# W1's column product in four pieces around one score product, and a shorter run of products on constants

## The chip, the cores and the metric

The kernel runs on one core of one Trainium2 chip. The metric is the device time of one execution in microseconds (us), from a few runs of the same program; one further execution was profiled.

## The reference

32 graphs of 512 nodes with 256 features go through two layers, each followed by a residual sum and a normalization. Layer 0 is a whole transformer block under a symmetric mask; layer 1 is attention under the plain mask.

```python
# layer 0: x is (32, 512, 256), adj is (32, 512, 512); 8 heads of 32
allowed = (adj > 0) | (adj.swapaxes(1, 2) > 0) | eye
q, k, v = split(x @ Wqkv.T + bqkv)
attn = softmax(where(allowed, (q / sqrt(32)) @ k.T, -inf))
x1 = layernorm(x + (attn @ v) @ Wo.T + bo) * g1 + be1
ff = relu(x1 @ W1.T + b1) @ W2.T + b2          # 256 -> 1024 -> 256
x = layernorm(x + (layernorm(x1 + ff) * g2 + be2))
# layer 1
w = softmax(where(adj == 0, -inf, (q @ k.T) / sqrt(32)))
x = layernorm(x + (w @ v) @ Wo.T + bo)
```

## The kernel before

A graph stays in on-chip memory from its load to its store. The work of the 32 graphs overlaps like a pipeline, and its order is written out by hand: `opening` (line 658) starts graphs a to e, `period` (line 1552) is called 26 times for the steady part, and `closing` (line 1855) ends the last ones. Inside these functions each line is one step of one graph (`a.scores(0, 5)` is the score product of block 5 of layer 0 for graph a). The steps are issued in the written order, and each engine and each issuing queue works through its own part of that order strictly; a step waits only for the data and the buffers it needs.

The attention of a layer is cut into eight blocks: two groups of four heads, times four tiles of 128 keys. For a block, `scores` (line 475) makes 16 TensorE records that write a tile `s` of 128 x 2048 in PSUM, `exp` (line 484, ScalarE) turns it into a tile `p` in on-chip memory, `masked` (line 488, VectorE) multiplies by the mask, and `product` (line 495) sums the values. There is only one tile `s`, so the score product of a block waits until the exponential before it has read the last one. `sums` (line 519) makes the row sums of the first graph on TensorE.

A product in 32-bit floats appears in the trace as two records, and so does its weight load.

Three steps of the opening matter here:

- `warm` (line 326) is a run of products on a tile of ones. Their result goes to a PSUM bank `psW` that nothing reads. They need the memset of the constants and nothing else, and stand ahead of the first transposes (`psT`, line 436), which need the first graph's `x`.
- `once(2)` (line 381) multiplies W1 by the column of the bias b2, into the PSUM bank `psB`: eight slices of 128 outputs, two halves of the contraction each, 64 equal columns, so 16 products in all with a weight load of 128 x 128 each. `once_out(2)` (line 394) later subtracts the result from b1, since b2 is added elsewhere and has to be taken out of the hidden layer's bias. W1 is loaded by `constants(6, 8)`, on SyncE's queue; the next cast of an adjacency matrix on GpSimd's queue (line 338) is made to wait for that load.
- `once(0)` and `once(1)` (line 374) are two short products of the same kind for the other biases.

The order around them is: score product of block 4, exponential and mask of block 4, score product of block 5, exponential of block 5, `once(2)`, score product of block 6, and then the mask and exponential steps of blocks 5 and 6, three value products and block 7. The step `sort` between them issues small copies on SyncE's queue for the next graph.

Of the kernel before, what the change touches and what calls it, by code (L numbers as in the profile page):

```python
# [27 lines left out]
def kernel(ctx: ExitStack, tc: tile.TileContext, t: dict, out: bass.AP):  # L28
# [14 lines left out]
    B, N, D = x.shape  # L43
    P = 128
    NQ = N // P
# [4 lines left out]
    NF = DFF // P  # L50
# [12 lines left out]
    ones = const.tile([P, HD], F32, name="ones")  # L63
# [87 lines left out]
    def plain(pools: ExitStack):  # L151
# [78 lines left out]
        class Graph:  # L230
# [17 lines left out]
            def bank(self, kind, n, shape):  # L248
# [4 lines left out]
                    self.tiles[key] = ps_d.tile([P, *shape], F32, tag=f"d_{next(slots['d'])}", name=name, bufs=1)  # L253
                return self.tiles[key]

            def direct(self, layer):

                return (self.b, layer) in ((0, 0), (B - 1, 1))
# [62 lines left out]

            def warm(self):

                ps = self.bank("W", (0,), [N])
                for _ in range(4):
                    nc.tensor.matmul(
                        ps,
                        ones[:, 0:1].to_broadcast([P, P]),
                        ones[:, 0:1].to_broadcast([P, N]),
                        start=True,  # L330
                        stop=True,
                    )
# [33 lines left out]
                loads = [nc.sync.dma_start(out=dst, in_=src) for dst, src in resident[a:b]]  # L366
                first[a] = loads[0]

            def once(self, i):

                if i < 2:
                    bv, ps = proj[i][3], self.bank("B", (i,), [D])
                    for k in range(ND):
                        nc.tensor.matmul(
                            ps, bv[:, k : k + 1].to_broadcast([P, P]), wo[i][:, k, :], start=(k == 0), stop=(k == ND - 1)
                        )
                    return
                ps = self.bank("B", (i,), [NF, P // 2])
                for f in range(NF):
                    for c in range(ND):  # L380
                        nc.tensor.matmul(  # L381
                            ps[:, f, :],
                            w1[:, c, f * P : (f + 1) * P],
                            b2_c[:, c : c + 1].to_broadcast([P, P // 2]),
                            start=(c == 0),
                            stop=(c == ND - 1),
                        )
# [125 lines left out]
            def sums(self, layer, hg):  # L513

                ps = self.bank("R", (layer, hg), [N])
                folded = [2 + hg] if not self.direct(layer) else range(hg * NQ, (hg + 1) * NQ)
                for k in folded:
                    for j in range(HPC):
                        nc.tensor.matmul(  # L519
                            ps[j * HD : (j + 1) * HD, :],  # L520
                            ones,
                            self.p(layer, k)[:, j, :],
                            start=(k == folded[0]),
                            stop=(k == folded[-1]),
                        )
# [132 lines left out]
        def opening(a, b, c, d, e):  # L658
# [52 lines left out]
            a.exp(0, 4)  # L711
            a.masked(0, 4)
            b.sort(0, 1, 0)
            a.scores(0, 5)
            a.exp(0, 5)
            a.once(2)
            a.scores(0, 6)
            b.sort(0, 1, 1)
            a.masked(0, 5)
# [2035 lines left out]
        with tc.manual_schedule():  # L2755
            opening(*graphs[: 5])
            for k in range(1, 27):
                period(*graphs[k : k + 5])
            closing(*graphs[27 : 32])

    with ExitStack() as pools:
        plain(pools)
# [166 lines left out]
    with ExitStack() as pools:  # L2929
# [3 lines left out]
        ps = ps_f.tile([1, 1], F32, name="ps_total")  # L2933
# [36 lines left out]
```

## Time and profile before

| What | us |
| --- | --- |
| median of 3 runs | 2995.37 |
| lowest and highest of them | 2994.23, 2999.42 |
| profiled execution, its own time | 2996.1 |
| span of its trace, first to last instruction | 2994.3 |
| TensorE busy in the span | 2968.1 (99%) |
| VectorE busy | 2700.5 (90%) |
| ScalarE busy | 1747.3 (58%) |
| GpSimd busy | 998.8 (33%) |
| constants (`psW`), first record to the transposes | 1.09 to 6.47 |
| score product of block 5 | starts 29.10 |
| W1's column product (`psB`, 32 records) | 31.04, takes 7.09 |
| score product of block 6 | starts 38.06 |
| first query or key product of the second graph | starts 57.29 |

Times inside the trace are counted from its first instruction. Engines carry short names: PE is TensorE's products, PEld its weight loads, DVE VectorE, ACT ScalarE, POOL GpSimd, SP SyncE. A line of the timeline gives the start, the duration, the engine, the line of the kernel, the operation, what it writes and reads, how many records were merged, and in brackets the idle time before the first of them and who ended it. A line of the stretches gives the borders, the length, the busy time and the number of records for PE, PEld, DVE, ACT and POOL, then the mean clock that TensorE was granted as a share of the full one, the busy share of the DMA engines and the GB/s moved.

### The profile page before, as it was taken

The page shows a single profiled execution, that of the slowest core. Times are in us where ns is not written, and L with a number is a line of the kernel's source. Part 1 is how long each engine was busy: PE and PEld are TensorE (multiplying, and loading weights), DVE is VectorE, ACT ScalarE, POOL GpSimd, SP SyncE. Part 2 cuts the span into 40 slices and gives each one's busy share as a digit, 9 for nine tenths or more (in the row PEclk, how much of TensorE's full clock was granted, in tenths as well). Part 3 has the DMA queues.
Part 4 walks back from the last instruction along what each step waited for, and adds up shares of the span by engine and source line. Part 5 has one row for each costly group of instructions (what it writes and reads, how often), then busy time and mean ns, then how long its engine had stood idle before and what let it go on. Part 6 is the DMA issues. An engine that isn't in the chain of part 4 may idle for free.

```text
span 2994.3 us, 83802 instructions
## 1 busy us (share of the span) xinstructions
PE 2968.1 (99%) x36842; PEld 1371.5 (46%) x36842; DVE 2700.5 (90%) x3585; ACT 1747.3 (58%) x2111; POOL 998.8 (33%) x1247
## 2 busy tenths in 40 slices
PE   9999999999999999999999999999999999999997
PEld 3444444454444544444544445444444444454443
DVE  4889999999999999999999999999999999998996
ACT  4555665556656556655566565566555665655554
POOL 0333333323333323333233333233332333333332
PEclk9999999999999999999999999999999999999999
DMA  7566767767667766666676677666766766667550
GB/s 151 115 123 135 139 134 132 132 128 146 130 133 134 131 132 138 134 133 127 130 147 130 133 135 131 132 137 135 133 122 133 145 132 133 137 122 141 100 111 27
DMA packets 276436, 387.08 MB, mean 129 GB/s; under 512 B 153248, under 2 KB 237344, under 8 KB 245792
## 3 DMA queue, kind: packets, MB, share of 16 engines
q0 software_dynamic: 35744, 260.59, 47.2%
q1 hardware_dynamic: 240320, 121.05, 18.4%
q8 instruction: 291, 4.77, 0.6%
q14 instruction: 81, 0.66, 0.1%
HBM read 72.23 MB, written 33.55 MB: 35 GB/s over the span
## 4 chain that ended last, share of the span: by engine, by line
PE 96%; DVE 2%; ACT 1%; DMA 0%; issue 0%; POOL 0%; SPq 0%; DVEq 0%; POOLq 0%
PE s L475 18%; PE acc L495 15%; PE psH L162 15%; PE psF L162 14%; PE psQK_None L162 11%; PE psV L162 7%; PE psO L162 7%; PE psQK L162 4%; PE psT L436 2%; PE psR L519 2%; ACT p L484 1%; DMA p<-p 0%; DVE p L488 0%; DVE st L602 0%; PE psB L381 0%
## 5 line engine op out<-in xcount | busy, mean ns | idle before, releaser
L484 ACT ACTIVATE p<-s 128x2048 f32<-128x2048 f32 x512 | 963.4, 1882 | 493.4 <-PE s L475 487.9
L488 DVE TENSOR_TENSOR p<-p,m 128x2048 f32<-128x2048 f32 x512 | 1162.5, 2278 | 38.9 <-ACT p L484 35.4
L475 PE MATMUL s<-qT,kT 32*64 32x512 f32 x8192 | 572.1, 614 | 8.3 <-ACT p L484 4.5
L495 PE MATMUL acc<-p,v 128*32 128x512 f32 x4096 | 508.9, 597 | 0.0
L162 PE MATMUL psH<-xT,w_L_gnn_W 128*32 128x256 f32 (+1 forms) x6296 | 471.0, 380 | 0.0
L162 PE MATMUL psF<-w_L_gnn_W,hT 128*32 128x256 f32 (+1 forms) x6896 | 459.9, 380 | 0.0
L610 POOL TENSOR_SCALAR rs<-mv 128x2 f32<-128x2 f32 (+1 forms) x320 | 210.9, 659 | 686.6 <-DVE mv L605 668.1
L511 DVE TENSOR_TENSOR p<-p,p 128x2048 f32<-128x2048 f32 x186 | 424.1, 2281 | 4.2 <-DMA p<-p 3.0
L162 PEld LDWEIGHTS psH<-xT,w_L_gnn_W 128*32 128x32 f32 (+1 forms) x6296 | 300.3, 118 | 199.5 <-issue 54.7
L611 POOL TENSOR_TENSOR rs<-rs,neg_half 128x2 f32<-128x2 f32 (+1 forms) x320 | 374.0, 1169 | 26.7
L162 PEld LDWEIGHTS psF<-w_L_gnn_W,hT 128*32 128x32 f32 (+1 forms) x6896 | 286.6, 115 | 184.7 <-ACT hT L646 31.4
L508 POOL DMA_DIRECT2D p<-p x186 | 171.3, 921 | 497.5 <-PE acc L495 441.6
L646 ACT ACTIVATE hT<-psH,c_L_gnn_b 128x256 f32<-128x256 f32 x512 | 212.1, 474 | 193.7 <-PE psH L162 184.6
L475 PEld LDWEIGHTS s<-qT,kT 32*64 32x64 f32 x8192 | 119.4, 130 | 316.0 <-issue 111.0
L535 POOL DMA_DIRECT2D p<-p x124 | 106.9, 862 | 439.8 <-DVE mv L605 193.2
L162 PE MATMUL psQK_None<-xT,w_L_gnn_Wqkv 128*32 128x512 f32 (+1 forms) x1988 | 243.1, 594 | 0.7 <-ACT xT L441 0.7
L162 PE MATMUL psO<-w_L_gnn_Wo,cT 128*32 128x256 f32 (+1 forms) x2728 | 240.1, 380 | 1.8 <-DVE cT L581 1.8
L495 PEld LDWEIGHTS acc<-p,v 128*32 128x32 f32 x4096 | 118.9, 110 | 258.5 <-issue 193.7
L162 PEld LDWEIGHTS psO<-w_L_gnn_Wo,cT 128*32 128x32 f32 (+1 forms) x2728 | 154.5, 123 | 97.2 <-issue 43.0
L441 ACT COPY xT<-psT 128x512 f32<-128x512 f32 x130 | 76.0, 585 | 200.7 <-PE psT L436 200.7
L631 ACT ACTIVATE x<-z,ms,rs 128x256 f32<-128x256 f32 x128 | 73.1, 596 | 158.8 <-DVE ms L615 155.7
L602 DVE BATCH_NORM_STATS2 st<-y 128x6 f32<-128x256 f32 x384 | 155.0, 422 | 6.5
(79 smaller groups left out, 2876.3 us busy)
## 6 DMA issues: line engine op xcount, KB each, us to landing
p<-p POOLq DMA_DIRECT2D x186, 1024.0 KB, 7.8
p<-p POOLq DMA_DIRECT2D x62, 512.0 KB, 5.9
x<-in_x_dram SPq DMA_DIRECT2D x32, 512.0 KB, 4.2
code<-in_adj_dram POOLq DMA_DIRECT2D x32, 512.0 KB, 6.2
m<-code SPq DMA_DIRECT2D x32, 512.0 KB, 4.9
kT<-v SPq DMA_DIRECT2D x248, 64.0 KB, 4.2
p<-p POOLq DMA_DIRECT2D x62, 256.0 KB, 6.3
part<-p SPq DMA_DIRECT2D x248, 64.0 KB, 2.0
```

Source lines behind the costliest of these rows:

```text
L162: nc.tensor.matmul(out[at], lhsT[:, at], rhs, start=start, stop=stop)
L475: nc.tensor.matmul(s[half * P // 2 : (half + 1) * P // 2, j, :], self.kT(layer)[at, hg, key : key + P // 2], self.qT(layer)[at, hg, :], st ...
L484: nc.scalar.activation(self.p(layer, k), self.at("s", (layer, k), [HPC, N]), AF.Exp, scale=SCALE)
L488: nc.vector.tensor_tensor(p, p, m[:, k % NQ, None, :].to_broadcast([P, HPC, N]), ALU.mult)
L495: nc.tensor.matmul(acc[j * HD : (j + 1) * HD, :], self.v(layer)[:, kc, h * HD : (h + 1) * HD], self.p(layer, k)[:, j, :], start=(kc == 0), ...
L508: nc.gpsimd.dma_start(out=self.p(layer, k), in_=self.p(layer, k + 1), accum_op=ALU.add)
L511: nc.vector.tensor_tensor(self.p(layer, dst), self.p(layer, a), self.p(layer, b), ALU.add)
L535: nc.gpsimd.dma_start(out=p[:rows], in_=p[rows : 2 * rows], accum_op=ALU.add)
L602: nc.vector.bn_stats(self.at("st", (n, i), [6]), self.y(n, i))
L610: nc.gpsimd.tensor_scalar(rs, self.mv(n)[:, a:b, 1:2], EPS, None, ALU.add)
L611: nc.gpsimd.tensor_tensor(rs, rs, neg_half[:, a:b, None], ALU.pow)
L646: nc.scalar.activation(self.hT(h)[:, f, :], ps[:, f % 2, :], AF.Relu, bias=b1[:, f : f + 1])
```

## The change

`warm` issues nine products of 128 columns where it issued four of 512. `once` takes a piece of a quarter: pieces 0 and 1 of W1's column product are issued ahead of the score product of block 5, pieces 2 and 3 right behind it. The arithmetic of W1's product is the same. `sums` gets a step of its range through a new method that always returns 1, which leaves it as it was.

```diff
+            def step(self, layer, hg):
+
+                return 1
+
...
             def warm(self):
 
-                ps = self.bank("W", (0,), [N])
-                for _ in range(4):
+                ps = self.bank("W", (0,), [P])
+                for _ in range(9):
                     nc.tensor.matmul(
                         ps,
                         ones[:, 0:1].to_broadcast([P, P]),
-                        ones[:, 0:1].to_broadcast([P, N]),
+                        ones[:, 0:1].to_broadcast([P, P]),
                         start=True,
                         stop=True,
                     )
...
-            def once(self, i):
+            def once(self, i, piece=0):
...
-                for f in range(NF):
+                for f in range(piece * NF // 4, (piece + 1) * NF // 4):
                     for c in range(ND):
                         nc.tensor.matmul(
                             ps[:, f, :],
...
-                folded = [2 + hg] if not self.direct(layer) else range(hg * NQ, (hg + 1) * NQ)
+                folded = [2 + hg] if not self.direct(layer) else range(hg * NQ, (hg + 1) * NQ, self.step(layer, hg))
...
             a.exp(0, 4)
             a.masked(0, 4)
             b.sort(0, 1, 0)
+            a.once(2, 0)
+            a.once(2, 1)
             a.scores(0, 5)
+            a.once(2, 2)
+            a.once(2, 3)
             a.exp(0, 5)
-            a.once(2)
             a.scores(0, 6)
             b.sort(0, 1, 1)
             a.masked(0, 5)
```

## The prediction

> **What bounds the kernel now.** I read the busy shares and the chain first, then the granted clock in stretches, then the opening instruction by instruction.
>
> ```profile
> PE 2968.1 (99%) x36842; PEld 1371.5 (46%) x36842; DVE 2700.5 (90%) x3585; ACT 1747.3 (58%) x2111; POOL 998.8 (33%) x1247
> ...
> PE 96%; DVE 2%; ACT 1%; DMA 0%; issue 0%; POOL 0%; SPq 0%; DVEq 0%; POOLq 0%
> ```
>
> TensorE (PE) sets the end. From the busy time by stretches, once the opening is over there is no gap left in which a late start could be made good, or an early one lost:
>
> ```profile
> 120.00:2920.00 2800.00, 2797.85 (x34895) 1293.66 (x34897) 2584.44 (x3407) 1658.27 (x2003) 959.71 (x1180) 1.00 0.68 132
> ```
>
> So a microsecond that the opening gives TensorE should come out at the end. The change touches two places of the opening. The first is where the clock halves. Columns: stretch, its length, then busy time of PE, PEld, DVE, ACT, POOL, then the granted clock. I found the borders by cutting the trace finer and finer:
>
> ```profile
> 25.31:28.72 3.41, 1.12 (x16) 0.24 (x16) 3.41 (x3) 2.61 (x3) 0.52 (x1) 1.00 1.43 275
> 28.72:42.38 13.66, 13.28 (x76) 8.16 (x80) 8.61 (x5) 4.08 (x3) 0.00 (x0) 0.50 0.58 156
> 42.38:45.79 3.41, 3.41 (x40) 0.76 (x36) 2.00 (x1) 0.70 (x1) 0.00 (x0) 1.00 1.06 316
> ```
>
> In the 3.41 us up to 28.72 TensorE works 1.12 us; then its clock is 0.50 for 13.66 us, four times 3.41. The timeline shows why it was idle and what then ran slowly:
>
> ```profile
> 25.95 1.12 PE L475 MATMUL s<-qT,kT 32*64 32x512 f32 x16 [0.81 <-ACT kT L465]
> 29.10 2.02 PE L475 MATMUL s<-qT,kT 32*64 32x512 f32 x16 [2.03 <-ACT p L484]
> 31.04 7.09 PE L381 MATMUL psB<-c_L_gnn_b,w_L_gnn_W 128*128 128x64 f32 x32
> 38.06 2.01 PE L475 MATMUL s<-qT,kT 32*64 32x512 f32 x16
> 40.01 3.93 PE L495 MATMUL acc<-p,v 128*32 128x512 f32 x24
> 43.87 1.11 PE L475 MATMUL s<-qT,kT 32*64 32x512 f32 x16
> ```
>
> The score product of block 5 waits 2.03 us for the exponential of block 4 (one score tile); only behind it come the 32 records of W1's column product (psB), which need nothing of it. The same score product takes 1.12 us at full clock and 2.02 us at half.
>
> The second place is the run on constants that opens TensorE's work:
>
> ```profile
> 1.09 5.54 PE L326 MATMUL psW<-ones 128*128 128x512 f32 x8 [1.09 <-POOL total L66]
> ...
> 3.81 0.33 PEld L326 LDWEIGHTS psW<-ones 128*128 128x128 f32 x1 [0.52 <-issue]
> 4.67 0.27 PEld L326 LDWEIGHTS psW<-ones 128*128 128x128 f32 x1 [0.52 <-issue]
> 5.18 0.19 PEld L326 LDWEIGHTS psW<-ones 128*128 128x128 f32 x1 [0.24 <-issue]
> 5.61 0.19 PEld L326 LDWEIGHTS psW<-ones 128*128 128x128 f32 x1 [0.24 <-issue]
> ...
> 6.47 1.03 PE L436 MATMUL psT<-ident,x 128*128 128x128 f32 x8
> ...
> 8.23 3.70 PE L162 MATMUL psQK_None<-xT,w_L_gnn_Wqkv 128*128 128x512 f32 x8 [0.73 <-ACT xT L441]
> ```
>
> Its loads are 0.86 us apart up to 4.67 and 0.43 us from 5.18: the array starts at half clock and gets the full one near 4.8, though the clock column, which has no record before that, says 1.00.
>
> **What the Trainium skill says.** "TensorE: Matmul & The Clock Gate", Part 1 (the HAM clock gate): half clock is the idle default, and a free-running window of 3413 ns decides it. The trace agrees with the window (13.66 us is four of them; 4.8 lies seven before 28.72). The page asks for an idle window before the clock drops; here one with 1.12 us of work was enough, so the measurement decides: the border lies above a third busy. As the window isn't tied to the kernel's start, other executions may cut it elsewhere. Same page, Part 4 (PE-mode transpose): transposes don't count as busy in the same way. In the closing, 2936.85 to 2940.27 holds 1.70 us of busy time, half of it transposes (0.33 + 0.55), and the clock is 0.50 in the 3.41 us after it; 2981.23 to 2984.64 holds 1.70 us of plain products, and the clock stays up in the 3.41 us after it. That fits, and puts the border between 33% and 50% of plain products.
>
> **The pieces, step by step.** Only TensorE's order changes; the same 32 records of psB run, 16 ahead of the score product of block 5 and 16 behind it. No other engine or queue has an instruction moved, no bank is taken in another order. One record costs 7.02/32 = 0.219 us at half clock (chain: 31.11 to 38.13). I halve it: 0.110; the upper bound is 0.129, from the transposes (1.03/8, the same 128x128 load with twice the columns). So 16 take 1.76 to 2.06 us; I take 1.76. In the old timeline's numbers, at full clock:
> - block 4's scores end at 27.0; 16 records to 28.8, where 2.03 us were idle. Block 5 still starts at 29.1, since ACT's exponential (1.88 us from 27.17) is what it waits for; with 0.129 it moves by under 0.1.
> - Block 5's scores, 1.05 (12.71 to 13.76), to 30.15; 16 records to 31.9. The exponential of block 5 runs 30.3 to 32.2, so block 6 starts at 32.25: a new gap of 0.34 us. Before: 38.06.
> - Block 6's scores to 33.3; 24 records of products at 3.46/32 each (50.40 to 53.86), 2.6, to 35.9; block 7 to 36.95 (its exponential before it ended at 35.4); 8 records, 0.9, to 37.8; sums 3.54 (45.80 to 49.34) to 41.35; psB of L374 1.06 to 42.4; products 3.46 to 45.9; sums 3.43 to 49.3. There the next graph's query product starts, before at 57.29.
>
> The sum is 8.0 us: 6.6 from the clock, 1.4 from the filled gap. Does cover hold? DVE's masking is one run from 23.74 to 37.04 (six tiles at 2.2), tied to its mask's landing, not to TensorE. Tiles 6 and 7 follow to 39.3 and 41.6, and their products start at 44.1 and 45.0. W1 has landed by 25.41, when the cast that waits for it is let go; b2's column, issued at 5.71, long before. The sync queue issues to 45.6 without waiting for TensorE, then waits 8.5 us for its products; that wait shrinks, and the later loads move with it. What is late next: exponential 5, for 0.34 us.
>
> **The constants, step by step.** Four products of 512 columns (8 records) become nine of 128 (18 records). At half clock one costs between 0.22 (a 128-column load, from psB) and 0.258 (twice a transpose's): 3.96 to 4.64 us, so the run ends between 5.0 and 5.7, not 6.63. x, issued at 0.74 with 4.1 us to land, is there at 4.8. Transposes to first query product took 6.63 to 8.23, 1.6: so 6.7 to 7.3, with Wqkv landing near 6.9 (1.24 + 5.7). Gain 0.9 to 1.3; I take 1.1. The bound on the other side: if the shorter run (4.0 to 4.6 us, little more than one window) fails to fill a window, transposes cost 1.0 more, of which the copies leave about 0.5, and the 3.7 us of query products run at half for at least one window, 1.7 lost: 1.1 gained becomes about 1.1 to 1.7 lost. With the window where this profile had it (1.42 to 4.83), the run covers it.
>
> **Sum.** The profiled execution took 2996.1 us (span 2994.3, 1.8 around it), 0.7 above the median of 2995.37. 2996.1 - 8.0 - 1.1 = 2987.0. A clock drop of one window in the closing (1.7 us) may come or go as the window falls; it stays in the range.
>
> **Rivals.**
> - The run on constants is too short, the clock stays at half into the query products: 2996.1 - 8.0 + 1.6 = 2989.7. For it: a run of little over one window fills a free-running one only where it happens to fit. Against: most fits leave a window largely busy.
> - The pieces count too little and the clock drops all the same. They stream 64 columns against a load of 128, and windows full of them at half clock (32.14 to 38.96) did not raise it. But then psB ends near 33.2 instead of 38.1 and the products raise the clock one or two windows earlier: gain 4.1 to 5.8 of the pieces, 2990 with the constants. Against: each window now also holds one score product, 1.05 us, and 0.9 us of streamed pieces, over 50%.
> - The gain is lost later, to a load or a mask tied to time: half of it, 2992. Against: TensorE never waits from 29.10 to 117.98.
> - Slower: the pieces meet W1's transfer. They had 5.6 us of slack (31.04 against 25.41); now they start at 25.9 to 27.0, 0.5 to 1.6 after it, and TensorE takes its instructions in order, so block 5's scores, its exponential and mask stand behind the wait. DMA is dense here (0.98 to 1.07 of the engines in 20 to 30 us). W1 landing 9 us later eats the gain, 16 us later (41) makes it over 0.2% slower: about 3003. It would take a transfer three times as long as seen.
>
> **How the numbers follow.** A measurement of this kernel tells about 0.2%, 6 us, from no change: faster means below 2989.4. Forecast 0.60; clock low at the start 0.18, a third of it still below 2989.4; pieces don't hold the clock 0.10, a fifth below; lost later 0.07; slower 0.05. Faster 0.65, same 0.30, slower 0.05. The range runs from 2984.5 (forecast less the closing's drop and the shorter bounds) to 2992 (the first three rivals).
>
> **What would show it.** Right: no stretch of clock 0.5 between 25 and 45 us, 16 records of psB in some 1.8 us on either side of block 5's scores, block 6's near 31 to 32, the next graph's query product near 48. The constants: transposes from 5.0 to 5.7, loads in the query products 0.43 apart. Wrong: loads 0.86 apart there; half clock after the pieces; a wait of psB for W1; new TensorE waits between 45 and 120 us.

## The result, and the profile after

The changed kernel takes 2986.60 us (median of 10 runs, 2984.82 to 2989.85); the kernel before, in 10 runs, 2994.96 us. The ratio is 0.9972, 95% interval 0.9962 to 0.9981: 0.28% faster, with 0.2 to 0.4% in the interval. The forecast was 2987.0. A few executions of several of the kernels here, the kernel before among them, took 5 to 16 us more than their median, and so medians are compared. The profiled execution took 2986.66 us, with a span of 2984.9 against 2994.3. The mean granted clock of every timed run is on record: 0.998 or 0.999 in the ten of the changed kernel, 0.994 to 0.997 in all 96 of the kernel before that were timed for the experiments.

The opening by TensorE's timeline (start, duration, what, records, wait before), in the changed kernel (most of the same steps stand four lines further down in it, L475 at L479 for one):

```profile
1.09 4.21 PE L330 MATMUL psW<-ones 128*128 128x128 f32 x18 [1.09 <-POOL total L66]
5.09 1.38 PE L440 MATMUL psT<-ident,x 128*128 128x128 f32 x8
7.20 3.70 PE L162 MATMUL psQK_None<-xT,w_L_gnn_Wqkv 128*128 128x512 f32 x8 [0.73 <-ACT xT L445]
...
24.91 1.12 PE L479 MATMUL s<-qT,kT 32*64 32x512 f32 x16 [0.81 <-ACT kT L469]
25.96 2.00 PE L385 MATMUL psB<-c_L_gnn_b,w_L_gnn_W 128*128 128x64 f32 x16
28.07 1.12 PE L479 MATMUL s<-qT,kT 32*64 32x512 f32 x16
29.11 2.00 PE L385 MATMUL psB<-c_L_gnn_b,w_L_gnn_W 128*128 128x64 f32 x16
31.22 1.12 PE L479 MATMUL s<-qT,kT 32*64 32x512 f32 x16
32.27 2.78 PE L499 MATMUL acc<-p,v 128*32 128x512 f32 x24
...
48.40 3.62 PE L162 MATMUL psQK_None<-xT,w_L_gnn_Wqkv 128*32 128x512 f32 x32
```

The score product of block 6 starts at 31.22 instead of 38.06, and each of these score products takes 1.12 us: none is slow any more. The next graph's query product starts at 48.40 instead of 57.29, 8.9 us earlier. The clock in the windows of 3.41 us around the pieces (length, PE, PEld, DVE, ACT, POOL busy, then the clock):

```profile
22.88:26.29 3.41, 2.60 (x31) 0.70 (x23) 3.27 (x4) 2.61 (x4) 0.52 (x1) 1.00 1.15 290
26.29:29.70 3.41, 3.31 (x36) 2.36 (x36) 3.41 (x3) 2.14 (x2) 0.00 (x0) 1.00 1.30 243
29.70:33.12 3.42, 3.31 (x37) 1.80 (x40) 3.42 (x3) 2.15 (x2) 0.00 (x0) 1.00 0.39 115
```

None of these windows is under 76% busy, and the clock stays 1.00. Now follow the 8.9 us to the end. The closing of the changed kernel:

```profile
2925.13 1.95 PE L162 MATMUL psO<-w_L_gnn_Wo,cT 128*128 128x256 f32 x8
...
2932.27 1.13 PE L162 MATMUL psQK<-xT,w_L_gnn_Wk 128*128 128x256 f32 x4 [0.68 <-ACT xT L445]
2933.24 1.03 PE L162 MATMUL psQK<-xT,w_L_gnn_Wq 128*128 128x256 f32 x4
2934.83 1.12 PE L479 MATMUL s<-qT,kT 32*64 32x512 f32 x16 [0.56 <-ACT qT L469]
```

And of the kernel before:

```profile
2932.95 1.96 PE L162 MATMUL psO<-w_L_gnn_Wo,cT 128*128 128x256 f32 x8
...
2940.10 1.92 PE L162 MATMUL psQK<-xT,w_L_gnn_Wk 128*128 128x256 f32 x4 [0.67 <-ACT xT L441]
2941.81 1.91 PE L162 MATMUL psQK<-xT,w_L_gnn_Wq 128*128 128x256 f32 x4
2944.29 1.12 PE L475 MATMUL s<-qT,kT 32*64 32x512 f32 x16 [0.56 <-ACT qT L465]
```

The psO products are 7.8 us apart: 1.1 us were given back on the way, 0.9 of it where an earlier psO product waits for cT. In the changed kernel:

```profile
2882.30 1.93 PE L162 MATMUL psO<-w_L_gnn_Wo,cT 128*32 128x256 f32 x32 [1.71 <-DVE cT L585]
```

In the kernel before:

```profile
2890.13 1.93 PE L162 MATMUL psO<-w_L_gnn_Wo,cT 128*32 128x256 f32 x32 [0.77 <-DVE cT L581]
```

This wait was 1.69 and 1.75 us in two more profiles of the changed kernel and 1.09 in one more of the kernel before, so it is no accident of one execution; why it grew was not followed up. The score products are 9.5 us apart: the two query and key products ahead of them ran at half clock in the kernel before (1.92 and 1.91 us) and do not here. So 9.4 us of span are 8.9 from the opening, 1.7 from the closing's clock, less 1.1 (rounded). The medians are only 8.4 us apart. The closing's clock depends on where the windows fall: it halved in five of all twelve traces (the kernel before twice, the constants alone, one piece in the gap, five constants) and held in seven.

### The profile page after: what moved, and what is told of

Its sections match the earlier page's. It is cut to its first block, busy times and chain, and to the rows that moved or that the text cites. A ratio compares the mean times of both kernels' runs of the same rounds, so it can differ in the third digit from the quotient of the medians.

```text
span 2984.9 us, 83822 instructions
## 1 busy us (share of the span) xinstructions
PE 2959.3 (99%) x36852; PEld 1369.0 (46%) x36852; DVE 2700.2 (90%) x3585; ACT 1748.9 (59%) x2111; POOL 1002.0 (34%) x1247
## 4 chain that ended last, share of the span: by engine, by line
PE 95%; DVE 2%; ACT 1%; DMA 1%; issue 0%; POOL 0%; SPq 0%; DVEq 0%; POOLq 0%
PE s L479 18%; PE acc L499 15%; PE psH L162 15%; PE psF L162 15%; PE psQK_None L162 11%; PE psV L162 7%; PE psO L162 7%; PE psQK L162 4%; PE psT L440 2%; PE psR L523 2%; ACT p L488 1%; DMA p<-p 1%; DVE st L606 0%; DVE p L515 0%; DVE y L603 0%
## 5 line engine op out<-in xcount | busy, mean ns | idle before, releaser
L479 PE MATMUL s<-qT,kT 32*64 32x512 f32 x8192 | 570.4, 613 | 6.8 <-ACT p L488 2.7
L479 PEld LDWEIGHTS s<-qT,kT 32*64 32x64 f32 x8192 | 119.2, 129 | 313.5 <-issue 109.3
```

The lines of the kernel that those rows point to most:

```text
L479: nc.tensor.matmul(s[half * P // 2 : (half + 1) * P // 2, j, :], self.kT(layer)[at, hg, key : key + P // 2], self.qT(layer)[at, hg, :], st ...
```

## The experiments

The kernels were timed beside the kernel before, on the same chip for each group; "before" is its median there. In the diffs, the base is the changed kernel; "constants as before" stands for four products of 512 columns.

**The pieces alone.** Constants as before.

```diff
-                ps = self.bank("W", (0,), [P])
-                for _ in range(9):
+                ps = self.bank("W", (0,), [N])
+                for _ in range(4):
...
-                        ones[:, 0:1].to_broadcast([P, P]),
+                        ones[:, 0:1].to_broadcast([P, N]),
```

> The pieces as in the changed kernel, the constants as before (4 products of 512 columns). Theory (the pieces keep the full clock through the gap, and the constants add about 1 us of their own): no half clock between 25 and 45 us, the second graph's first query product near 49.3 instead of 57.29, time 8.0 us below the kernel before, about 2987. Rival (the early start of the whole opening by the shorter constants is what moved the idle gap against the clock's windows and kept the clock): the clock still halves after 28 us and at most 1.4 us are gained.

2986.89 us, before 2995.12, ratio 0.9971 (0.9961 to 0.9981). The trace has no half clock in the opening. Its query product starts at 50.26; its first transposes started at 7.30 instead of 6.47, so the pieces themselves gave 7.03 + 0.83 = 7.9 us (57.29 less 50.26, and the later start). The mean clock is 0.999 in all nine runs. The rival falls: the pieces carry the gain without the constants.

**The constants alone.** The whole product behind block 5.

```diff
-            a.once(2, 0)
-            a.once(2, 1)
             a.scores(0, 5)
+            a.exp(0, 5)
+            a.once(2, 0)
+            a.once(2, 1)
             a.once(2, 2)
             a.once(2, 3)
-            a.exp(0, 5)
```

> The constants as in the changed kernel, W1's column product whole and behind block 5 as before. Theory: the first query product starts 1.0 us earlier, the clock still halves once in the opening for two to four windows of 3.41 us, time 0.5 to 1.5 us below the kernel before. Rival (constants decide): no half clock, 7 to 9 us gained.

2993.71 us, before 2995.12, ratio 0.9995 (0.9986 to 1.0003). The clock stretches of its trace:

```profile
26.77:30.18 3.41, 1.93 (x24) 1.12 (x24) 3.41 (x2) 2.14 (x2) 0.00 (x0) 1.00 1.22 230
30.18:40.42 10.24, 10.24 (x59) 6.38 (x61) 8.12 (x5) 3.05 (x2) 0.00 (x0) 0.50 0.64 166
```

The clock halves for three windows. Three of the 13 runs took 2988.2 to 2988.4 us, all others 2993.3 or more. The mean granted clock on record is 0.999 in these three and 0.996 or 0.997 in the other ten. So with the constants alone the clock held in some executions and fell in most, and where it held the time was some 5 us shorter, about what three windows at half clock cost (half of 10.24 us). No trace of one of the three was taken.

**The whole product ahead of block 5.** Constants as before.

```diff
             a.once(2, 0)
             a.once(2, 1)
+            a.once(2, 2)
+            a.once(2, 3)
             a.scores(0, 5)
-            a.once(2, 2)
-            a.once(2, 3)
             a.exp(0, 5)
```

> Constants as before; all four pieces of W1's column product ahead of the score product of block 5, so that the gap before block 5 is overfilled and an idle gap of about 2.1 us arises before block 6, behind one score product and dense products after it. Theory (a window with little product work halves the clock, wherever it is): block 5 starts near 30.9 instead of 29.1, block 6 near 34.1 instead of 32.3; 1.8 us lost against the split pieces; if a window falls on the new gap the clock halves for one window and 1.7 us more are lost. 6.2 or 4.5 us below the kernel before. Rival (only that the product stands ahead of block 5 matters, not the split): the full 8.0 us.

2989.41 us, before 2995.12, ratio 0.9988 (0.9977 to 0.9999). The trace shows the gap moved by one block, and the clock falling there for one window:

```profile
31.79:35.21 3.42, 1.52 (x23) 0.41 (x27) 3.42 (x2) 2.15 (x2) 0.00 (x0) 1.00 0.42 119
35.21:38.62 3.41, 3.41 (x24) 0.82 (x16) 3.41 (x3) 1.58 (x1) 0.00 (x0) 0.50 0.75 208
```

Its timeline: block 5 starts at 30.54 and block 6, after 2.04 us of waiting, at 33.69; the 24 value products behind it take 4.48 us instead of 2.78. The query product starts at 52.57, 4.7 us before the old time, as the case with one halved window said. The split matters: with all records ahead, TensorE has nothing to do beside the exponential of block 5.

**Mere filling.** Constants as before; the first half of the product runs in the gap as well and again in its old place.

```diff
             a.once(2, 0)
             a.once(2, 1)
             a.scores(0, 5)
+            a.exp(0, 5)
+            a.once(2, 0)
+            a.once(2, 1)
             a.once(2, 2)
             a.once(2, 3)
-            a.exp(0, 5)
```

> Constants as before; the first half of W1's column product is issued twice, once ahead of block 5 as mere filling and again with the whole product behind block 5 where it was. Theory (6.6 of the 8.0 us are the clock's): the clock stays full, block 6 starts near 34.2, 1.9 us later than with the split pieces; about 6.1 us below the kernel before although TensorE does 16 records more. Rival (the gain is useful work moved into the gap): nothing gained, 0 to 1.8 us lost.

2990.73 us, before 2995.12, ratio 0.9988 (0.9980 to 0.9996); the profiled execution took 2989.16. TensorE's timeline of it:

```profile
26.88 2.00 PE L385 MATMUL psB<-c_L_gnn_b,w_L_gnn_W 128*128 128x64 f32 x16
28.98 1.12 PE L479 MATMUL s<-qT,kT 32*64 32x512 f32 x16
30.03 3.79 PE L385 MATMUL psB<-c_L_gnn_b,w_L_gnn_W 128*128 128x64 f32 x32
33.75 1.11 PE L479 MATMUL s<-qT,kT 32*64 32x512 f32 x16
```

The 16 extra records do no new work, and yet block 6 starts at 33.75 instead of 38.06 and the query product at 50.93, 6.4 us earlier (0.1 of it because this execution's opening began earlier). The old place of the product costs 3.7 us where it had cost 7.0. So most of the gain in the opening is the clock's; useful work in the gap is worth only the rest. The timed median is 4.4 us below the kernel before, with an interval of 1.2 to 6.0 us that just misses the 6.1 that were expected; the clear gain still rules out the rival.

**One piece in the gap.** Constants as before.

```diff
             a.once(2, 0)
-            a.once(2, 1)
             a.scores(0, 5)
+            a.once(2, 1)
             a.once(2, 2)
```

> Constants as before; only one of the four pieces (8 records, 1.0 us) ahead of block 5, three behind it, so that 1.0 us of the 2.03 us gap stays idle. Theory (the clock falls when too little product work lies in one window): the window on the gap holds one score product and one piece, more than the window that halved the clock in the kernel before; the clock holds, block 6 starts 0.9 us later than with two pieces on either side, about 7 us below the kernel before. If the clock falls in spite of the one piece: 2 to 4 us below, and the border lies above such a window.

2987.98 us, before 2994.49, ratio 0.9978 (0.9969 to 0.9986). The window on the gap and the next:

```profile
26.03:29.44 3.41, 2.15 (x24) 1.20 (x24) 3.41 (x3) 2.57 (x3) 0.00 (x0) 1.00 1.27 240
29.44:32.85 3.41, 3.41 (x37) 2.60 (x38) 3.41 (x2) 1.88 (x1) 0.00 (x0) 1.00 0.41 119
```

One microsecond of light products, with 1.0 us still idle, was enough in this execution: 63% busy, and the clock holds. The timed gain is 6.5 us, where about 7 were expected.

**A run on constants that is too short.** Five products instead of nine.

```diff
-                for _ in range(9):
+                for _ in range(5):
```

> The changed kernel with five products of 128 columns in the run on constants instead of nine (about 2.2 us of work at half clock, less than one window of 3.41 us). Theory (the run is there to lift the clock, and nine are about the least that does): the run ends near 3.3 us, the transposes start with x near 4.8 us but run at half clock, the query products start near 8 us instead of 7.2 and run at half for at least a window; 2 to 4 us above the changed kernel, 4 to 6 below the kernel before. Rival (the constants only delay the start): as fast as the changed kernel or up to 0.3 us faster.

2988.38 us, before 2994.49, ratio 0.9979 (0.9970 to 0.9988). Loads of the first query product, in time:

```profile
9.36 0.34 PEld L162 LDWEIGHTS psQK_None<-xT,w_L_gnn_Wqkv 128*128 128x128 f32 x1 [0.52 <-issue]
10.21 0.34 PEld L162 LDWEIGHTS psQK_None<-xT,w_L_gnn_Wqkv 128*128 128x128 f32 x1 [0.52 <-issue]
11.07 0.34 PEld L162 LDWEIGHTS psQK_None<-xT,w_L_gnn_Wqkv 128*128 128x128 f32 x1 [0.52 <-issue]
11.92 0.28 PEld L162 LDWEIGHTS psQK_None<-xT,w_L_gnn_Wqkv 128*128 128x128 f32 x1 [0.52 <-issue]
12.44 0.19 PEld L162 LDWEIGHTS psQK_None<-xT,w_L_gnn_Wqkv 128*128 128x128 f32 x1 [0.24 <-issue]
```

They are 0.85 apart until 11.9: the array is at half clock until 12.1. The transposes start at 4.88, when x has landed, but the first score product only at 14.24, against 11.68 in the changed kernel: 2.6 us lost. The run is there to lift the clock. In the timed runs the loss is smaller than the 2 to 4 us that were expected: the median is 1.3 to 1.8 us above those of the changed kernel (2986.60 and 2987.06 us, timed in other groups), and the intervals of the ratios overlap.

**Both kernels profiled once more**, for another cut of the windows.

> The kernel before, profiled once more. Theory (free-running windows of 3.41 us cut each execution elsewhere, but the idle gap before block 5 is long enough for most cuts): the clock halves again after 27 to 31 us, for two to four windows; the end of the run on constants moves by up to 1.5 us with the window.

> The changed kernel, profiled once more. Theory: no half clock between 25 and 45 us, wherever the window falls; the transposes start between 5.0 and 5.7 us; if the window does not fit the short run on constants, the query products start at half clock and the opening is 1 to 3 us later than in the first profile.

The kernel before halves again, from 30.16 to 43.81, after a window of 40%:

```profile
26.74:30.16 3.42, 1.39 (x24) 0.40 (x32) 3.42 (x2) 2.22 (x2) 0.00 (x0) 1.00 1.11 218
30.16:43.81 13.65, 13.65 (x80) 8.02 (x68) 8.42 (x5) 3.75 (x2) 0.00 (x0) 0.50 0.62 178
```

Its constants end 0.7 us later than in the first profile (transposes at 7.18). The changed kernel again has no half clock in the opening; its query product starts at 48.61.

**The closing filled.** Five products on constants into the gaps ahead of and behind the last transposes, and the changed kernel beside it.

```diff
+            e.fill(2)
             e.transpose(2, 1)
...
+            e.fill(3)
             e.query_key(1, 1, 0, 1, wide=True)
```

> The changed kernel, with five products of 128 columns on constants added in the idle gaps of the closing around the last transposes: two ahead of the last graph's second transposes of layer 1, three ahead of its key product after them (10 records, about 1.1 us, into the score tile that is empty there). Theory (too little product work in a window halves the clock, and some executions have such a window in the closing, which costs 1.65 us there): the clock stays full to the last products in every execution, nothing is delayed; the median falls by up to 1.7 us against the changed kernel, by as much as the share of executions that had the halving. Rival (the closing's halving is rare or is not from the gaps): no difference, or 0.1 to 0.5 us lost to the fillings.

> The changed kernel once more, beside the one with the filled closing on the same chip. 2986 to 2987 us; no half clock in the opening; in the closing the clock halves or not as the window falls.

2986.66 and 2987.06 us, before 2994.57; ratios 0.9980 (0.9970 to 0.9990) and 0.9976 (0.9970 to 0.9983). No difference that can be told. The closing of the changed kernel kept its clock in all three of its profiles without the fillings. Two kernels with the same closing lost it there, the one with one piece and the one with five constants, after windows of 50% and 54%, so the fillings have something to save in some executions; the timed runs don't show it. None of the versions is faster than the changed kernel by more than the noise.

Not every execution of these two kernels keeps its clock: in five of their 35 runs the mean clock is 0.997, and these five took 2992.4 to 2998.5 us. None of them was profiled. Three of them have the closing filled, so the gaps that were filled are hardly the cause. The shorter run on constants is no likely one either: the 11 runs with five constants have no such case, and the 13 with mere filling, on the old run, have one. Where the clock fell in them stays open.

## Why the prediction was right

**The pieces: right.** Forecast 8.0 us; 7.9 with the old constants. The steps held one by one: block 6 at 32.25 less the earlier start is 31.2, measured 31.22; the new gap before it shrank from 0.34 to 0.25 us (29.11 plus 1.86 is 30.97), since 16 records take 1.86 us, not 1.76: 32 of them run in 3.72 us in the two experiments with whole products, 0.116 each, inside the bounds of 0.110 and 0.129. Masks, context copies and the sync queue did not hold TensorE up in the opening, as argued.

**The split of the gain: right.** Forecast 6.6 for the clock and 1.4 for the gap; mere filling kept about 6.2, which leaves 1.7 of the 7.9.

**The constants: right in the opening, lost on the way to the end.** The first exponential starts at 13.8 to 14.8 us in the six traces with the old run (mean 14.20) and at 12.8 to 13.3 in the five with nine products (13.04): 1.16 us, forecast 1.1. But the timed medians with the old run and the new are 2986.89 and 2986.60 to 2987.06, and the traces show that the microsecond did not reach the end: with the pieces alone the query product starts 1.86 us later than in the changed kernel (50.26 against 48.40), and the psO product of the closing 0.4 us earlier (2924.75 against 2925.13). Some 0.9 us of that were made up near 2770 us and 0.8 us at the wait for cT near 2882 (0.94 against 1.71 us). So the step "once the opening is over there is no gap left in which a late start could be made good" failed for a term of this size. The pieces' 8 us did come out: 8.2 by the medians. Why the waits on the way differ was not followed up.

**W1's transfer: right, and closer than it looks.** The profile names W1 as what the first load of the pieces waited for:

```profile
25.96 1.86 PEld L385 LDWEIGHTS psB<-c_L_gnn_b,w_L_gnn_W 128*128 128x128 f32 x16 [0.81 <-DMA w_L_gnn_W<-in_L_gnn_W_dram]
```

Its 0.81 us of idle time is no loss: the first load of the second half, at 29.11, shows the same 0.81 us with no transfer to wait for. W1 had landed at 25.30 (issued at 19.77, 5.5 us to land). In the four traces with pieces and nine constants it landed 0.2 to 0.7 us ahead of this load; the forecast had put 0.5 to 1.6.

**The border of the clock: wrong at its upper end.** The prediction set it between 33% and 50% of plain products. Over the twelve traces, windows at full clock in the opening and closing that were up to 40% busy were always followed by half clock, those of 58% and more never, and between 44% and 56% both occur. The window of 56%, in the kernel with the constants alone (26.77 to 30.18), held no transposes and still lost the clock. The lightest window around the pieces had 76% in the changed kernel, so the forecast did not depend on where the border lies.

**"Transposes don't count": not shown.** The Trainium skill, "TensorE: Matmul & The Clock Gate", Part 4 (PE-mode transpose), says that they don't count as busy in the same way. The prediction read the closing that way: a window of 50%, half of it transposes, lost the clock, and one of 50% psO products kept it. Over all the traces transposes are not the ones that stand out. Windows of psO products kept the clock at 44% and 49%. Windows of the closing with transposes in them lost it at 50%, four times out of four, and kept it at 59%. But the window of 56% above, of score products and W1's, lost it without any. So the share at which the clock falls differs by what fills the window. Two closings come close to it, the first of the pieces alone, the second of five constants; their windows differ by 0.02 us of work, each with 0.88 us of transposes in it, and only the first kept the clock:

```profile
2928.32:2931.73 3.41, 1.85 (x9) 0.96 (x7) 2.29 (x7) 2.05 (x4) 2.35 (x5) 1.00 0.00 0
2931.73:2935.15 3.42, 2.71 (x24) 1.67 (x24) 1.11 (x3) 1.04 (x3) 0.00 (x0) 1.00 0.01 2
```

```profile
2930.48:2933.90 3.42, 1.83 (x9) 0.95 (x7) 2.30 (x7) 2.07 (x4) 2.33 (x5) 1.00 0.00 0
2933.90:2937.31 3.41, 3.29 (x8) 2.52 (x8) 1.09 (x3) 0.54 (x2) 0.00 (x0) 0.50 0.01 2
```

For lifting the clock, transposes can't count for nothing. In the kernel with the filled closing the nine constants end at 5.1, and two windows follow each other:

```profile
0.00:3.30 3.30, 2.21 (x10) 2.21 (x11) 0.23 (x1) 1.28 (x1) 0.82 (x9) 1.00 0.26 71
3.30:6.71 3.41, 3.41 (x18) 3.30 (x16) 0.00 (x0) 0.52 (x1) 0.00 (x0) 1.00 1.13 348
```

The clock column has no record before the end of the second and reads 1.00; the loads show the clock. The first, with 2.21 us of constants, did not lift it: loads stay 0.21 us apart until 6.4, as they are from the start. The second holds constants and transposes in about equal parts, and the clock is lifted at its end, at 6.71: the query products that follow take 3.70 us, the full rate. If transposes counted for nothing, it would have been half empty, emptier than the first. The rival with too short constants did not occur in any of the five traces with nine of them.

**The sum: right, in part by luck.** 1.7 us from the closing's clock, which the text left in its range, and 1.1 us given back on the way, which it put at nothing, nearly cancel in the profiled pair. That the forecast came within 0.4 us of the median owes something to this. The chances, as they are listed, add up to 0.68 for "faster" (0.60, 0.06 and 0.02), not 0.65; nothing hangs on it.

## What to carry to other kernels

Look for a stretch of lower granted clock before anything else when TensorE is the bound, and then at the 3.4 us ahead of it: an idle gap of 2 us there cost about 6.2 us behind it, three times itself. Independent products, even light or useless ones, belong in such a gap, and on both sides of the wait if the next one is as long; issued all at once they only moved the gap here. Shortening the run that lifts the clock from four products of 512 columns to nine of 128 started the opening 1 us earlier, but the time shows nothing of it; with five of 128, less than a window, the opening lost 2.6 us in its trace. A microsecond gained early is not yet one at the end, even where TensorE is 99% busy: follow it through the trace.

## What the runs showed of the hardware

Lifting the clock asked for more than keeping it. A window 80% busy (5.29 to 8.70 in the kernel with five constants) did not lift it, nor did 2.21 us of constants in one window (65% of 3.41 us, in the kernel with the filled closing); windows 58 to 65% busy kept it. In the closing, windows of 83% and more at half clock lifted it. Nearly half of the 80% were transposes, so that window alone does not tell whether share or kind decides.

Windows full of W1's column product at half clock (128-column loads, 64 columns streamed) did not lift it either. This one, of the kernel before, holds nothing else, and the clock stays at half behind it:

```profile
32.14:35.55 3.41, 3.41 (x18) 3.41 (x18) 3.41 (x3) 0.95 (x1) 0.00 (x0) 0.50 0.33 84
```

(The next window, to 38.96, which the prediction counted as full of them too, is a quarter score product.) The window shown is 100% busy by the profile, which models the ends of the products; how much of it counts towards the clock is not known. So the price of a gap hung on what came behind it: after an idle gap of 2.0 us the clock was down for three or four windows where W1's product followed whole (the kernel before in both profiles, and the constants alone), and for one where value products followed (the whole product ahead of block 5).
